# Softmax denominators in a cross attention with heads of 64: VectorE folds the sums of exps to 64 partitions, and one product takes two chunks of heads

## The chip, the cores and the metric

The kernel runs on one core of one Trainium2 chip. Its engines work side by side, each through its own queue in order: TensorE (PE in the profile; PEld is its weight load), VectorE (DVE), ScalarE (ACT), GpSimd (POOL) and SyncE (SP), which here issues DMAs. The metric is the device time of one execution in microseconds (us), the median of several runs. Everything is computed in fp32.

## The reference, cut to what matters

A decoder of two layers works on x of 8 batches, 256 tokens and 256 features. Each layer adds a self attention, a cross attention over a context of 256 rows by 512 features, and a routed feed-forward part. The change lies in the cross attention of the second layer, which has 16 heads of 64 and one more key and value, the same for every head and batch ("null"):

```python
q = _split_heads(jnp.einsum('bnd,df->bnf', x, Wq))          # x is layer-normed
kv = jnp.einsum('bmc,cf->bmf', context, Wkv)
k, v = jnp.split(kv, 2, axis=-1)
k, v = (_split_heads(k), _split_heads(v))
k = jnp.concatenate((nk, k), axis=-2)                       # nk, nv: null_kv, broadcast
v = jnp.concatenate((nv, v), axis=-2)
q = q * scale
sim = jnp.einsum('bhid,bhjd->bhij', q, k)
attn = jax.nn.softmax(sim, axis=-1)
out = jnp.einsum('bhij,bhjd->bhid', attn, v)
out = out.transpose(0, 2, 1, 3).reshape(b, -1, INNER)
out = jnp.einsum('bnf,fd->bnd', out, Wout)                  # then a layer norm with scale and bias
```

The denominator of the softmax, for each head and query, is the sum over 256 keys of exp(score), plus the exp of the null key's score.

## The kernel before

The stage is the function `null_cross_attention`, one entry per batch (the loop `for b in range(B)` at L1473). The 16 heads lie as eight chunks (`nc8`) of two heads, `g` = 0 and 1, 64 features each. Two chunks make a block, so an entry has four blocks; `c2` counts chunks in steps of two.

**Inside `weighted` (L1331).** For a chunk, `exp_scores` makes the scores transposed, keys on the partitions: PE multiplies `kT` and `qT` into `stx` (L1339; 256 keys are two tiles of 128, `kt`), ScalarE takes the exp into `pTx` (L1343), and GpSimd adds the two key tiles (L1345), so that `both` holds, on 128 partitions, sums of two keys' exps, for two heads by 256 queries. What is left is a sum over the 128 partitions. PE does it (`sums`, L1353): for each head a product with weights `hot8[:, c, :]`, a matrix of 128 by 64 that is 1 in column c and 0 elsewhere, so that the sum lands in row c of the tile `den`; rows 0 to 63 take the heads with g = 0, rows 64 to 127 those with g = 1, and the eight chunks accumulate into one PSUM tile. So an entry has 16 of these products, 128 x 64 weights and 256 columns each; the profile counts two records to a product.

The block loop (L1367) keeps PE ahead: it issues the scores of block c2 + 2, then `sums` of block c2 - 2, then the products of the exps with the values (`ox`, L1377) of block c2. `ox` is copied out of PSUM into `oT` by ScalarE for c2 = 0 and 4 and by VectorE for c2 = 2 and 6 (L1385). The last block's `sums` are left over as `rest`.

**After it.** PE transposes the next entry's normed x and the routed rows' (`tr`, L283), and makes the next entry's keys, values and queries with the seven-product scheme `seven` (L1239; k7, v7 and q7 are generators whose every `next` issues a piece of products, their sums and copies). `rest` stands behind the first piece of k7 (L1503). Then `reciprocals` (L1394): VectorE adds the null key's exp to den (`rx`) and takes the reciprocal, four DMAs on SyncE write it to DRAM and read it back spread over the partitions (`rs`), GpSimd multiplies `oT` by it (`divide`, L1428), and PE multiplies by `Wout` (`wo`).

**Buffers.** `pTx` has four, `both` has four, the PSUM tag `mm` three (ox, tr, the z tiles of `seven`, wo and nps take them in turn), `sc` two of two banks (scores and `seven`), and `den` the one bank of `op`. `oT` has one.

**Who sets the order.** The order on every engine is that of a scheduler that follows the program with its dependences; from L1493 to the end of an entry (`manual_schedule`) PE keeps the order as written. In the entries before the last two the second layer norm of an entry is made one entry ahead (`xn`), beside that of the routed rows (`xne`), which VectorE and GpSimd do at the beginning of an entry (L251 to L260).

Of the kernel before, what the change touches and what calls it, by code (L numbers as in the profile page):

```python
# [28 lines left out]
F32 = mybir.dt.float32  # L29
# [4 lines left out]
ALU = mybir.AluOpType  # L34
# [4 lines left out]
P = 128  # L39
B, S, D = 8, 256, 256  # L40
# [4 lines left out]
XH, XD = 16, 64  # L45
# [110 lines left out]
def plain(  # L156
# [4 lines left out]
    nc = tc.nc  # L161
# [402 lines left out]
    work = first.enter_context(tc.tile_pool(name="aw", bufs=2))  # L564
# [200 lines left out]
    nc8 = XH // 2  # L765
# [26 lines left out]
    def tables_x(wd, wq_x, wout_x, nkrow, nvcol):  # L792


        wn = wd.tile([P, 2, 2, XD], F32, name="wn")
        nc.gpsimd.memset(wn, 0.0)
        for k in range(2):
            byk = work.tile([P, XH, XD], F32, tag="pT", name="byk", bufs=4)
            nc.vector.tensor_tensor(
                byk,  # L800
                wq_x[:, k, :].rearrange("p (h d) -> p h d", d=XD),
                nkrow.unsqueeze(1).to_broadcast([P, XH, XD]),
                ALU.mult,
            )
            nc.vector.tensor_reduce(
                wn[:, k, :, :nc8], byk.rearrange("p (c g) d -> p g c d", g=2), AX.X, ALU.add
            )

        own = wd.tile([P, 2], F32, name="own")
        nc.vector.tensor_reduce(own, ident.rearrange("p (g w) -> p g w", g=2), AX.X, ALU.add)  # L810
        nc.vector.tensor_tensor(own, own, nvcol.to_broadcast([P, 2]), ALU.mult)
        nvs = work.tile([P, nc8, P], F32, tag="pT", name="nvs", bufs=4)
        nc.gpsimd.memset(nvs, 0.0)
        for c in range(nc8):
            nc.vector.tensor_copy(nvs[:, c, c : c + XD + 1 : XD], own)
        nvw = wd.tile([P, D], F32, name="nvw")
        ps = mm.tile([P, 2, S], F32, tag="mm", name="nvw")
        for c in range(nc8):
            nc.tensor.matmul(ps[:, 0, :], nvs[:, c, :], wout_x[:, c, :], start=c == 0, stop=c == nc8 - 1)
        nc.vector.tensor_copy(nvw, ps[:, 0, :])  # L820

        hot = wd.tile([P, nc8, XD], F32, name="hot8")
        nc.gpsimd.memset(hot, 0.0)
        nc.gpsimd.memset(hot.rearrange("p c w -> p (c w)")[:, 0 : nc8 * XD : XD + 1], 1.0)
        return wn, nvw, hot

    def beside(n):
# [15 lines left out]
    before = units[0].prepare()  # L843
# [13 lines left out]
    for n, u in enumerate(units):  # L857
        done = n
        if n == 1:
            expert_tables()  # L860
        if n == 3:
            slot_tables()
        if n == 2:
            nc.sync.dma_start(wqkv1, a["l1_wqkv"].rearrange("(c p) f -> p c f", p=P))
            nc.sync.dma_start(wo1, a["l1_wo"].rearrange("(c p) f -> p c f", p=P))
            nc.sync.dma_start(sin1, a["sin_halves"].rearrange("(t p) d -> p t d", p=P))
        if n + 2 < len(units):
            units[n + 2].load()

        if n + 1 < len(units) and units[n + 1].__class__ is SelfAttention and units[n + 1].layer == 1:  # L870
            while len(ready) <= units[n + 1].b // 2:
                next(experts_at)
        if n == len(units) - 1:
            wd, ctxs, wproj, wkv_x, wq_x, wout_x, nkrow, nvcol, lns, lnb = wx
            wn, nvw, hot8 = tables_x(wd, wq_x, wout_x, nkrow, nvcol)
        side = beside(n)
        m = (units[n - 1].pieces[1] if n else 0) + (units[n + 1].pieces[0] if n + 1 < len(units) else 0)
        made = 0
        for i, _ in enumerate(u.core()):
            while made < min(m, -(-m * (i + 1) // 7)):  # L880
                next(side)
                made += 1
            next(experts_at, None)
        for _ in side:
            pass
        opening.close()
        if len(ready) == B // 2 and wx is None:
            wx = weights_x()
# [281 lines left out]
    def null_cross_attention(phase):  # L1170
        work = phase.enter_context(tc.tile_pool(name="d2", bufs=2))
# [156 lines left out]
            nc.scalar.activation(en, nps[:, 0, :], AF.Exp, scale=scale)  # L1328
            return en

        def weighted(kT, v, qT):  # L1331


            def exp_scores(c):
                st = scp.tile([P, 2, 2, S], F32, tag="sc", name="stx")
                for kt in range(2):
                    for g in range(2):
                        rows = slice(XD * g, XD * (g + 1))
                        nc.tensor.matmul(  # L1339
                            st[:, g, kt, :], kT[rows, c, bass.ts(kt, P)], qT[rows, c, :], start=True, stop=True  # L1340
                        )
                pT = work.tile([P, 2, 2, S], F32, tag="pT", name="pTx", bufs=4)
                nc.scalar.activation(pT, st, AF.Exp, scale=scale)  # L1343
                both = work.tile([P, 2, S], F32, tag="both", name="both", bufs=4)
                nc.gpsimd.tensor_tensor(both, pT[:, :, 0, :], pT[:, :, 1, :], ALU.add)  # L1345
                return pT, both

            oT = work.tile([P, nc8, S], F32, tag="oT", name="oT", bufs=1)
            den = op.tile([P, S], F32, tag="o", name="den")

            def sums(c, both):
                for g in range(2):
                    nc.tensor.matmul(  # L1353
                        den[XD * g : XD * (g + 1), :],
                        hot8[:, c, :],
                        both[:, g, :],
                        start=c == 0,
                        stop=c == nc8 - 1,
                        skip_group_check=True,
                    )  # L1360

            def block(c2):
                return [exp_scores(c2 + i) for i in range(2)]


            ahead, before = block(0), []
            for c2 in range(0, nc8, 2):  # L1367
                now = ahead
                if c2 + 2 < nc8:
                    ahead = block(c2 + 2)  # L1370
                for i, both in enumerate(before):
                    sums(c2 - 2 + i, both)
                o = mm.tile([P, 2, S], F32, tag="mm", name="ox")
                for i, (pT, _) in enumerate(now):
                    for kt in range(2):
                        for g in range(2):
                            nc.tensor.matmul(  # L1377
                                o[XD * g : XD * (g + 1), i, :],
                                v[:, kt, 2 * (c2 + i) + g, :],
                                pT[:, g, kt, :],  # L1380
                                start=kt == 0,
                                stop=kt == 1,
                                skip_group_check=True,
                            )
                (nc.vector.tensor_copy if c2 % 4 else nc.scalar.copy)(oT[:, c2 : c2 + 2, :], o)  # L1385
                before = [both for _, both in now]

            def rest():
                for i, both in enumerate(before):
                    sums(nc8 - 2 + i, both)  # L1390

            return oT, den, rest

# [67 lines left out]
        _, xnT = layernorm_T(0, work, mm, 1)  # L1461
        ctxT, kT, v, qT = context(0), key_room(), value_room(), query_room()
# [10 lines left out]
        for b in range(B):  # L1473
            more = b + 1 < B
            if more:
                ctxT = context(b + 1)
            oT, den, rest = weighted(kT, v, qT)
            if more:
                _, xnT = layernorm_T(b + 1, work, mm, 1)
                if b:  # L1480
# [15 lines left out]
            if more:  # L1496
                of_x = sums_of_rows(xnT, 1, "swq", True)
                kT, v, qT = key_room(), value_room(), query_room()
                k7 = seven("k7", of_ctx, w_terms(kv_blocks, 0), kT, False)
                v7 = seven("v7", of_ctx, w_terms(kv_blocks, 1), v, True)  # L1500
                q7 = seven("q7", of_x, w_terms(q_blocks, 0), qT, False)
                next(k7)
                rest()  # L1503
            rs, old = reciprocals(b, den, en), en
            if b == 1:
                in_range()
# [2 lines left out]
                routing_tables(late)  # L1509
            if more:  # L1510

                for made in (k7, k7, v7, k7, k7, k7, v7, v7, q7, v7, q7, v7, v7, q7):
                    next(made)
            else:
                first = hidden_shared(0, pair, lambda n: spare()[:, 0, :n])
                for i in range(4):
                    next(first)
                    if i == 0:
                        routed_scores(b - 1)
                shared["of_w"] = sums_of_shared(*(sums.tile([P, full * P], F32, name=f"tws{i}") for i in range(4)))  # L1520
# [1242 lines left out]
```

## Time and profile before

| what | us |
|---|---|
| median of 3 runs (1362.37 to 1363.51) | 1363.12 |
| the profiled execution, its own time | 1360.92 |
| its span, first to last instruction | 1359.2 |
| first entry of the stage (650.69 to 710.01) | 59.32 |
| entries two to seven, each | 59.81 or 59.82 |
| PE busy in the third entry (769.83 to 829.64) | 59.49 of 59.81 |
| VectorE, ScalarE, GpSimd busy in it | 20.13, 17.99, 19.49 |
| L1353, all den products (256 records) | 34.3, 386 ns one record |
| L1345, all adds of GpSimd (64) | 82.0, 1308 ns one |

Times of instructions are given as they stand in the timeline: start from the beginning of the span, length, engine, line, operation, what is written from what is read, the shape, and how many were joined to one line; a bracket at the end says how long the engine was idle before, and what ended that. PE's matmuls are pipelined, so a line's length runs over into the next line's, and what a group costs is read from start to start. The TensorE clock that was granted is 0.996 of full speed over the span.

### The profile page before, as it was taken

The numbers are of one execution on the slowest core, as the hardware profiler recorded it, in microseconds if no ns is written. First come the engines' busy times: TensorE is split into PE (matmuls) and PEld (weight loads), VectorE is DVE, ScalarE is ACT, GpSimd is POOL, SyncE is SP. The second block draws the span as 40 slices with busy tenths as digits, with TensorE's granted clock in tenths as the row PEclk, the third lists the DMA queues.
The fourth block names the chain that finished last, engine by engine and source line by source line (L and its number), as shares of the span: only waits on it lengthen the run. The fifth ranks groups of instructions, "written<-read, shape, count | busy, mean of one in ns | idle before, by whom it ended". The sixth has DMA issues, their size and how long they took to land.

```text
span 1359.2 us, 30873 instructions
## 1 busy us (share of the span) xinstructions
PE 1325.6 (98%) x13180; PEld 918.7 (68%) x13180; DVE 562.6 (41%) x1622; ACT 477.5 (35%) x768; POOL 385.3 (28%) x481
## 2 busy tenths in 40 slices
PE   6999999999999999999999999999999999999998
PEld 3666766766766756665767676676767657788884
DVE  5343463463465655344333323242332547322223
ACT  2455544444444333431323323132332323022221
POOL 4232052052034244220324324141433512300004
PEclk8999999999999999999999999999999999999999
DMA  9970010000000005000111010201101111689954
GB/s 310 341 234 11 15 25 7 11 25 1 1 9 1 2 10 194 18 1 9 27 30 33 17 33 17 48 13 37 33 16 33 65 32 44 260 351 398 400 195 127
DMA packets 46930, 116.71 MB, mean 86 GB/s; under 512 B 8272, under 2 KB 30400, under 8 KB 42432
## 3 DMA queue, kind: packets, MB, share of 16 engines
q1 hardware_dynamic: 38912, 92.74, 20.2%
q0 software_dynamic: 5152, 18.89, 3.8%
q10 hardware_dynamic: 2720, 3.02, 0.6%
q8 instruction: 106, 1.74, 0.5%
q14 instruction: 40, 0.33, 0.1%
HBM read 104.00 MB, written 27.93 MB: 97 GB/s over the span
## 4 chain that ended last, share of the span: by engine, by line
PE 86%; DVE 4%; issue 2%; POOL 2%; ACT 1%; DMA 1%; SPq 0%; ACTq 0%; POOLq 0%; DVEq 0%
PE st L334 11%; PE o L366 10%; PE h L274 6%; PE v L274 6%; PE k L274 5%; PE wo L274 4%; PE ox L1377 4%; PE stx L1339 4%; PE qk L274 3%; PE out L1751 3%; PE out L1568 3%; PE h L961 3%; PE tr L283 3%; PE q L274 2%; PE den L1353 2%
## 5 line engine op out<-in xcount | busy, mean ns | idle before, releaser
L366 PE MATMUL o<-pT,padv 128*64 128x256 f32 (+1 forms) x1536 | 171.6, 365 | 1.2 <-POOL pT L346 1.2
L343 ACT ACTIVATE pT<-st 128x1024 f32<-128x1024 f32 (+1 forms) x128 | 110.5, 915 | 88.9 <-PE st L334 88.1
L366 PEld LDWEIGHTS o<-pT,padv 128*64 128x64 f32 x1536 | 103.1, 137 | 52.7 <-issue 9.6
L334 PE MATMUL st<-qm,kT 64*128 64x256 f32 (+1 forms) x1024 | 117.2, 367 | 0.9 <-DVE qm L312 0.6
L334 PEld LDWEIGHTS st<-qm,kT 64*128 64x128 f32 x1024 | 90.1, 189 | 26.2 <-issue 15.8
L1345 POOL TENSOR_TENSOR both<-pTx 128x512 f32<-128x512 f32 x64 | 82.0, 1308 | 46.0 <-ACT pTx L1343 38.9
L274 PE MATMUL h<-xrT,w 128*64 128x128 f32 (+1 forms) x1936 | 87.1, 250 | 1.4 <-issue 1.4
L274 PEld LDWEIGHTS h<-xrT,w 128*64 128x64 f32 x1936 | 84.6, 137 | 4.1 <-issue 2.0
L343 ACT ACTIVATE pT<-st,kbias 128x1024 f32<-128x1024 f32 x64 | 68.0, 1112 | 28.8 <-PE st L334 28.7
L1343 ACT ACTIVATE pTx<-stx 128x1024 f32<-128x1024 f32 x64 | 62.1, 1021 | 42.3 <-PE stx L1339 40.3
L256 POOL TENSOR_TENSOR lnrs<-lnve,mhalf 128x2 f32<-128x2 f32 x48 | 34.2, 715 | 146.0 <-DVE lnve L254 95.1
L954 DVE TENSOR_TENSOR midr<-sl,h 128x128 f32<-128x128 f32 x102 | 29.4, 288 | 101.3 <-PE h L274 67.0
L334 PE MATMUL st<-qm,memk 64*128 64x256 f32 x512 | 68.8, 393 | 0.4
L953 ACT ACTIVATE sl<-h 128x128 f32<-128x128 f32 (+1 forms) x114 | 35.3, 310 | 95.7 <-PE h L274 56.7
L1339 PE MATMUL stx<-qTx,kTx 64*128 64x256 f32 x512 | 64.3, 391 | 2.5 <-ACT pTx L1343 2.5
L274 PE MATMUL qk<-l_wqkv,xnT 128*64 128x512 f32 x256 | 62.6, 610 | 0.7 <-ACT xnT L286 0.7
L346 POOL TENSOR_SCALAR_AFFINE_SELECT pT<-pT 128x512 f32<-128x512 f32 x64 | 39.6, 638 | 80.9 <-ACT pT L343 77.6
L1377 PE MATMUL ox<-pTx,vx 128*64 128x256 f32 x512 | 61.1, 381 | 0.0
L1339 PEld LDWEIGHTS stx<-qTx,kTx 64*128 64x128 f32 x512 | 46.1, 186 | 20.3 <-ACT pTx L1343 7.2
L274 PE MATMUL wo<-wout_x,oT 128*64 128x256 f32 x512 | 58.0, 379 | 0.0
L334 PEld LDWEIGHTS st<-qm,memk 64*128 64x128 f32 x512 | 48.0, 186 | 14.8 <-issue 4.7
L1428 POOL TENSOR_TENSOR oT<-oT,rs 128x512 f32<-128x512 f32 x30 | 37.2, 1272 | 64.4 <-DMA rs<-rd 64.4
(368 smaller groups left out, 2270.1 us busy)
## 6 DMA issues: line engine op xcount, KB each, us to landing
w<-packs SPq DMA_DIRECT2D x22, 1408.0 KB
w<-packs SPq DMA_DIRECT2D x22, 768.0 KB
rs<-rd SPq DMA_DIRECT2D x16, 512.0 KB
packs<-L_ffn_w_eDF SPq DMA_DIRECT2D x8, 704.0 KB
packs<-L_ffn_w_eDF SPq DMA_DIRECT2D x8, 640.0 KB
packs<-L_ffn_w_eFD SPq DMA_DIRECT2D x8, 640.0 KB
ctxT<-ctx_T SPq DMA_DIRECT2D x8, 512.0 KB
wkv_x<-L_xattn_Wkv POOLq DMA_DIRECT2D x1, 4096.0 KB, 15.4
```

What stands on the lines that cost most here:

```text
L274: nc.tensor.matmul(out[h], lhsT[:, h], rhs, start=start, stop=stop, skip_group_check=True)
L283: nc.tensor.transpose(ps[:, c, t * P : (t + 1) * P], rows[:, t, c * P : (c + 1) * P], ident)
L334: nc.tensor.matmul(st[:, g, i, :n], kT[rows, c, bass.ts(kt, P)], qm[rows, 2 * mq + i, c, q0:], start=True, stop=True,)
L343: nc.scalar.activation(pT[:, :, :, :n], st[:, :, :, :n], AF.Exp, scale=scale, **kb)
L366: nc.tensor.matmul(o[64 * i : 64 * i + 64, mq, q0:], v_pad[:, kt, 4 * c + 2 * mq + i, 2 * g : 2 * g + 2, :], pTs[kt][:, g, i, : S - q0], s ...
L961: nc.tensor.matmul(h, shared["ws13"][:, c, lo : lo + P], shared["xnT"][:, c, bass.ts(q, 2 * S)], start=c == 0, stop=c == 1)
L1339: nc.tensor.matmul(st[:, g, kt, :], kT[rows, c, bass.ts(kt, P)], qT[rows, c, :], start=True, stop=True)
L1343: nc.scalar.activation(pT, st, AF.Exp, scale=scale)
L1345: nc.gpsimd.tensor_tensor(both, pT[:, :, 0, :], pT[:, :, 1, :], ALU.add)
L1377: nc.tensor.matmul(o[XD * g : XD * (g + 1), i, :], v[:, kt, 2 * (c2 + i) + g, :], pT[:, g, kt, :], start=kt == 0, stop=kt == 1, skip_group ...
L1568: nc.tensor.matmul(ps, mid[:, i, lo : lo + P], w2[:, i, :], start=i == 0, stop=i == NFC - 1)
L1751: nc.tensor.matmul(ps[h], mid[:, i, h], sets[k % len(sets)][1][:, i, :], start=i == 0, stop=i == NFC - 1, skip_group_check=True,)
```

## The change

Three things change in `weighted` and around it; the last entry (`folds` = `more` = False) is kept as it was but for the names of its buffers.

1. In the first seven entries VectorE adds the lower 64 partitions of `both` to the upper 64. The first chunk of a block goes to partitions 0 to 63 of a tile `folded`, the second to 64 to 127, so one `folded` holds a block of two chunks.
2. One product per head and block then takes both chunks: the weights `hot[1]` have 1 in one column for the lower 64 partitions and in the next column for the upper 64. That makes 8 products an entry instead of 16, of the same shape. The tables become a strip of 72 columns, of which each product reads a window of 64.
3. The products of a block are issued one block of scores later: behind the scores of block c2 + 2 stand now those of block c2 - 4. Two blocks are left over at the end; `rest` is called twice, behind the first and behind the second piece of k7.

`both` has two buffers instead of four, and `folded` three. In the last entry the chunks of a block take a buffer of `both` and one of `folded`, without a fold.

```diff
-        hot = wd.tile([P, nc8, XD], F32, name="hot8")
-        nc.gpsimd.memset(hot, 0.0)
-        nc.gpsimd.memset(hot.rearrange("p c w -> p (c w)")[:, 0 : nc8 * XD : XD + 1], 1.0)
+        hot = [wd.tile([P, XD + nc8], F32, name=f"hot{i}") for i in range(2)]
+        for v in hot:
+            nc.gpsimd.memset(v, 0.0)
+        nc.gpsimd.memset(hot[0][:, nc8 - 1 : nc8], 1.0)
+        for i in range(2):
+            nc.gpsimd.memset(hot[1][XD * i : XD * (i + 1), nc8 - 2 + i : nc8 - 1 + i], 1.0)
...
-        def weighted(kT, v, qT):
+        def weighted(kT, v, qT, folds):
...
-                both = work.tile([P, 2, S], F32, tag="both", name="both", bufs=4)
+                return pT
+
+            def room(odd):
+                if odd:
+                    return work.tile([P, 2, S], F32, tag="folded", name="folded", bufs=3)
+                return work.tile([P, 2, S], F32, tag="both", name="both", bufs=2)
+
+            def add(pT, both):
                 nc.gpsimd.tensor_tensor(both, pT[:, :, 0, :], pT[:, :, 1, :], ALU.add)
-                return pT, both
+                return both
+
+            def sum_block(pTs):
+                if not folds:
+                    return [add(pT, room(i)) for i, pT in enumerate(pTs)]
+                folded = room(1)
+                for i, pT in enumerate(pTs):
+                    both = add(pT, room(0))
+                    nc.vector.tensor_tensor(folded[XD * i : XD * (i + 1)], both[:XD], both[XD:], ALU.add)
+                return [folded]
...
-            def sums(c, both):
-                for g in range(2):
-                    nc.tensor.matmul(
-                        den[XD * g : XD * (g + 1), :],
-                        hot8[:, c, :],
-                        both[:, g, :],
-                        start=c == 0,
-                        stop=c == nc8 - 1,
-                        skip_group_check=True,
-                    )
+            def sums(c2, of):
+                for i, v in enumerate(of):
+                    at = nc8 - (2 if folds else 1) - c2 - i
+                    for g in range(2):
+                        nc.tensor.matmul(
+                            den[XD * g : XD * (g + 1), :],
+                            hot[folds][:, at : at + XD],
+                            v[:, g, :],
+                            start=c2 + i == 0,
+                            stop=c2 + 2 == nc8 and i + 1 == len(of),
+                            skip_group_check=True,
+                        )
...
-            ahead, before = block(0), []
+            ahead = block(0)
+            made = [(0, sum_block(ahead))]
             for c2 in range(0, nc8, 2):
                 now = ahead
                 if c2 + 2 < nc8:
                     ahead = block(c2 + 2)
-                for i, both in enumerate(before):
-                    sums(c2 - 2 + i, both)
+                if c2 >= (4 if folds else 2):
+                    sums(*made.pop(0))
+                if c2 + 2 < nc8:
+                    made.append((c2 + 2, sum_block(ahead)))
                 o = mm.tile([P, 2, S], F32, tag="mm", name="ox")
...
             def rest():
-                for i, both in enumerate(before):
-                    sums(nc8 - 2 + i, both)
+                sums(*made.pop(0))
...
-            oT, den, rest = weighted(kT, v, qT)
+            oT, den, rest = weighted(kT, v, qT, more)
...
-                next(k7)
-                rest()
+                for _ in range(2):
+                    next(k7)
+                    rest()
...
-                for made in (k7, k7, v7, k7, k7, k7, v7, v7, q7, v7, q7, v7, v7, q7):
+                for made in (k7, v7, k7, k7, k7, v7, v7, q7, v7, q7, v7, v7, q7):
                     next(made)
```

More of the change, by code (lines that the diff above doesn't have):

```diff
@@ L874, in plain @@
             wd, ctxs, wproj, wkv_x, wq_x, wout_x, nkrow, nvcol, lns, lnb = wx
-            wn, nvw, hot8 = tables_x(wd, wq_x, wout_x, nkrow, nvcol)
+            wn, nvw, hot = tables_x(wd, wq_x, wout_x, nkrow, nvcol)
         side = beside(n)
@@ L1370, in weighted @@
                     ahead = block(c2 + 2)
-                for i, both in enumerate(before):
-                    sums(c2 - 2 + i, both)
+                if c2 >= (4 if folds else 2):
+                    sums(*made.pop(0))
+                if c2 + 2 < nc8:
+                    made.append((c2 + 2, sum_block(ahead)))
                 o = mm.tile([P, 2, S], F32, tag="mm", name="ox")
-                for i, (pT, _) in enumerate(now):
+                for i, pT in enumerate(now):
                     for kt in range(2):
@@ L1385, in weighted @@
                 (nc.vector.tensor_copy if c2 % 4 else nc.scalar.copy)(oT[:, c2 : c2 + 2, :], o)
-                before = [both for _, both in now]
             def rest():
-                for i, both in enumerate(before):
-                    sums(nc8 - 2 + i, both)
+                sums(*made.pop(0))
             return oT, den, rest
```

## The prediction

> **What bounds the kernel now.** The page's head and first part come first.
>
> ```profile
> span 1359.2 us, 30873 instructions
> PE 1325.6 (98%) x13180; PEld 918.7 (68%) x13180; DVE 562.6 (41%) x1622; ACT 477.5 (35%) x768; POOL 385.3 (28%) x481
> ```
>
> PE is busy all the way, so each product that is really taken away is worth its issue time, unless PE then finds something unready. The change touches one stage, the eight entries of cross attention with heads of 64, so next I read PE's timeline in one steady entry (the third; it starts at 769.83 and the fourth at 829.64, and entries two to seven are alike within 0.01 us).
>
> ```profile
> 776.00 2.00 PE L1339 MATMUL stx<-qTx,kTx 64*128 64x256 f32 x16
> 777.93 1.08 PE L1353 MATMUL den<-both,hot 128*64 128x256 f32 x8
> 778.84 1.90 PE L1377 MATMUL ox<-pTx,vx 128*64 128x256 f32 x16
> 780.67 2.00 PE L1339 MATMUL stx<-qTx,kTx 64*128 64x256 f32 x16
> 782.60 1.08 PE L1353 MATMUL den<-both,hot 128*64 128x256 f32 x8
> 783.51 1.90 PE L1377 MATMUL ox<-pTx,vx 128*64 128x256 f32 x16
> 785.24 1.03 PE L1353 MATMUL den<-both,hot 128*64 128x256 f32 x8
> 786.10 1.90 PE L1377 MATMUL ox<-pTx,vx 128*64 128x256 f32 x16
> 787.93 0.66 PE L283 MATMUL tr<-ident,xn 128*128 128x128 f32 x4
> ```
>
> The reader is to see starts without gaps: a den group costs 0.91, 0.91 and 0.86 us from start to start (two records to a product). Next, the two engines that the change loads, VectorE and GpSimd, in the same entry:
>
> ```profile
> 774.70 1.27 POOL L1345 TENSOR_TENSOR both<-pTx 128x512 f32<-128x512 f32 x1
> 774.77 1.36 DVE L260 TENSOR_SCALAR xne<-x,lnmv,lnrs 128x256 f32<-128x256 f32 x1 [0.68 <-POOL lnrs L256]
> 776.05 0.42 DVE L260 TENSOR_SCALAR xne<-x,lnmv,lnrs 128x256 f32<-128x256 f32 x1
> 776.80 6.18 POOL L1345 TENSOR_TENSOR both<-pTx 128x512 f32<-128x512 f32 x5
> 780.79 0.69 DVE L1385 COPY oT<-ox 128x512 f32<-128x512 f32 x1 [4.32 <-PE ox L1377]
> ```
>
> The same VectorE instruction takes 1.36 us when it starts just behind a GpSimd add, ending 0.16 after it, and 0.42 without one. The adds themselves step by (6.18 - 1.27) / 4 = 1.23. The last entry already holds what the change will bring, VectorE instructions with two inputs in SBUF during those adds:
>
> ```profile
> 1079.18 1.89 DVE L973 TENSOR_TENSOR tws<-ws 128x640 f32<-128x640 f32 x1
> 1080.36 1.84 POOL L1345 TENSOR_TENSOR both<-pTx 128x512 f32<-128x512 f32 x1
> 1081.00 1.88 DVE L973 TENSOR_TENSOR tws<-ws,tws 128x640 f32<-128x640 f32 x1
> 1082.17 1.86 POOL L1345 TENSOR_TENSOR both<-pTx 128x512 f32<-128x512 f32 x1
> ```
>
> They take turns. An add ends 1.13 after the VectorE instruction ahead of it (1081.07 to 1082.20), and the VectorE instruction 0.68 after that add (1082.88). VectorE alone does four 512-wide ones like this:
>
> ```profile
> 614.12 2.48 DVE L1217 TENSOR_TENSOR tw<-wkv_x 128x512 f32<-128x512 f32 x4
> ```
>
> That is 0.68 each, a step of 0.60 where they run on.
>
> **Part one, the products removed.** In seven entries den goes from 16 products to 8. Ahead of tr the group at 777.93 goes (0.91), and those at 782.60 and 785.24 are halved (0.43 each): 1.77. The switch from stx straight to ox costs 0.05 (the ox group at 774.12 lasts 1.88 to the next start, others 1.83), so PE wants tr 1.71 earlier, at 786.22. Behind tr the old group of 0.86 becomes two halves of 0.43: nothing. Unhindered that is 7 x 1.71 = 12.0 us.
>
> **Part two, the folds added.** Eight VectorE instructions an entry, 64 partitions by 512. Half the partitions do not make one shorter: L954 takes 690 ns at 64x512 and 686 at 128x512. So 0.68 alone. Behind a running add I scale the 0.68 of 640 elements: 0.68 x 512 / 640 = 0.55 after the add's end; the bounds are 0.55 and 0.72 (0.68 and a handover of 0.04: L1235 starts at 790.07, 0.04 after the end of L1234, which it reads). I take 0.55, since L973 is the same kind of instruction against the same adds. In the changed program's order each fold also waits for the fold ahead, so a fold behind a fold costs 0.72, at the least 0.60. The tile both has two buffers instead of four: the add of chunk c waits for the fold of chunk c - 2. After a fold, the next fold is there in 0.04, GpSimd's add only in 0.14 (L1447 at 771.32, after a L1446 that ends at 770.76 + 0.42), so I let the fold go first.
>
> **What is queued behind them.** VectorE's order becomes: two xne, folds 0 to 5, the copy of ox of chunks 2 and 3, folds 6 and 7, the copy of ox of chunks 6 and 7. The tag mm has three buffers, so tr (ox two blocks on, then tr) needs the bank of that first copy, and k7z that of the second. In the old order the first copy ran at 780.79. Followed from the rows (ends):
>
> - fold 0: the second xne ends at 776.47, VectorE starts 0.08 earlier, 777.07. Add 1, issued at 776.80: +1.13, 778.20. Add 2: +1.23, 779.43. Fold 1: +0.55, 779.98. Fold 2: +0.72, 780.70.
> - Add 3 781.83, add 4 783.06, fold 3 783.61, fold 4 784.33. PE wants fold 3 (second den) at 784.0: met.
> - Add 5 785.46, add 6 786.69, fold 5 787.24, copy (0.04 + 0.69) 787.97. With 0.05 to PE, tr starts at 788.02 instead of 786.22; before it was 787.93.
>
> The copy that PE now waits for eats 1.80 of 1.71: such an entry loses 0.09. ScalarE stays covered: exp 7 needs add 3 (781.83), and its scores come at about 781.9. The second copy ends at 790.6; k7z wants its bank at 788.02 + 3.68 - 0.43 = 791.27: met.
>
> The first and the seventh entry differ in when the adds start. In the first, at 653.03, nothing of a layer norm stands ahead: adds 0 and 1 end by 655.52, folds 0 and 1 by 656.79, and with pairs of 1.13 + 1.23 + 0.55 + 0.72 = 3.63 fold 5 ends at 664.05 and the copy at 664.78, ahead of the 667.02 at which PE wants tr. It keeps 1.71. In the seventh add 1 ends at 1016.57; fold 1 1017.84, fold 5 1025.10, copy 1025.83: tr 0.40 late, and k7z, by the second copy at 1029.46, another 0.38. It keeps 1.71 - 0.78 = 0.93. Sum: 5 x 0.09 - 1.71 - 0.93 = **-2.2 us**. Against the median of 1363.12 that is 1360.9; the profiled execution itself was 1360.92 with a span of 1359.2, 2.2 below the median, and I apply the difference, not the span.
>
> A step of 0.60 between folds instead of 0.72 would bring the copy 3 x 0.12 forward: 1.8 us in five entries, and 0.3 in the seventh. That is the low edge of this case, -4.3.
>
> [...]
>
> **Part three, denominators a block later.** The last two den products move behind k7z and half of the sw products, so rx starts at about 795.4 instead of 791.83. Behind it on VectorE, SyncE's queue and GpSimd: reciprocal, four DMAs, the product with en, four products with rs; nobody else stands in those queues then. They ended at 807.47, now at 811.1, and PE wants them at 817.7: covered with 6.6 to spare. Without that cover it would cost 3.6 an entry. The last entry keeps its instructions and order on PE and VectorE, and the tables' fills on GpSimd lie far ahead of their use (first den at 658.7): nothing for both.
>
> **Rivals.**
> 1. The folds do not hold up the adds. Adds then step by 1.23, fold 5 ends at 782.98 + 0.72, the copy at 784.43, before PE wants the bank: all of 12.0 is kept, 1351.1. For it: L1385 copies during adds at 0.69, unslowed; but it has one input, in PSUM. Against it: L973. Half-way cases lie here too. 0.15.
> 2. Strict turns: after each fold the add goes first, a pace of 0.55 + 0.14 + 1.27 = 1.96 a chunk. Fold 5 ends at 779.98 + 4 x 1.96 = 787.82, tr at 788.60, +0.67 in five entries, +0.51 in the seventh, -1.71 in the first: +2.2, 1365.3. For it: L973's own turns are of this form. Against: there the add had no wait on VectorE. 0.20.
> 3. Slower: the two engines hide nothing from each other, since both buffers are two and every handover is a wait: 0.04 + 0.68 + 0.14 + 1.27 = 2.13 a chunk. Fold 1 ends at 779.43 + 0.72, fold 5 at 788.67, tr at 789.45: +1.52 in five entries and in the seventh, -1.06 in the first: +8.1, **1371**. It decides from a pace of about 2.0 a chunk on. Against it: the 0.68 and 1.13 of L973, where the starting time is hidden. 0.18.
>
> **How the numbers follow.** 0.47 for the forecast, 1360.9 (1358.8 to 1363 on its own). What the measurement can tell from no change is 0.2%, 2.7 us: the forecast lies 0.20 on the faster side of that and 0.27 inside, rival 1 is faster, rival 2 0.12 inside and 0.08 slower, rival 3 slower. Faster 0.35, same 0.39, slower 0.26. The range leaves out most of rival 1 and of rival 3: 1354 to 1367.5.
>
> **What would show it.** Right: adds beside folds at 1.8 us or so, in pairs; L283's tr behind a gap of 1.8 us in entries two to six that ends with VectorE's oT, none in the first; wo without a wait. Wrong: adds still at 1.27 and no gap (rival 1); one fold between any two adds (2); folds ending a full 0.7 after an add (3). A GpSimd wait of wo would undo part three.

## The result, and the profile after

| what | before | after |
|---|---|---|
| median, us, side by side on one chip (10 runs each) | 1363.24 (1361.6 to 1366.87) | 1368.64 (1367.14 to 1370.18) |
| ratio, with its 95% interval | | 1.0038 [1.0028, 1.0048] |
| profiled execution, us (its span) | 1360.92 (1359.2) | 1368.88 (1367.1) |
| mean granted TensorE clock of the profile | 0.996 | 0.990 |

The change made the kernel 5.4 us slower. First the page of after:

```profile
span 1367.1 us, 30772 instructions
PE 1320.0 (97%) x13068; PEld 914.8 (67%) x13068; DVE 630.7 (46%) x1678; ACT 479.1 (35%) x768; POOL 396.6 (29%) x484
```

PE is busy for 5.6 us less, in a span that is 7.9 us longer, so it stands still for longer, and part of what it still does runs slower. The third entry shows both. In the kernel after, L1356 is GpSimd's add, L1367 the fold, L1377 the den products, L1405 ox and L1413 its copy. PE's timeline there (start, length, engine, line, operation; it starts at 768.98):

```profile
783.10 0.60 PE L1377 MATMUL den<-folded,hot 128*64 128x256 f32 x4
783.53 1.90 PE L1405 MATMUL ox<-pTx,vx 128*64 128x256 f32 x16
787.43 0.66 PE L283 MATMUL tr<-ident,xn 128*128 128x128 f32 x4 [2.01 <-DVE oT L1413]
787.93 0.87 PE L283 MATMUL tr<-ident,xne 128*128 128x128 f32 x4
788.73 3.32 PE L274 MATMUL k<-ctxT,wkv_x 128*64 128x128 f32 x32
```

PE stands still for 2.01 us ahead of tr, until VectorE's copy of ox is done; tr starts 18.45 into the entry, 0.35 later than before (18.10). And the 32 records of k behind it, which take 1.97 in an entry that runs at full clock, take 3.32. The table by stretches says why. Its columns are the stretch, its length, the busy time with the instructions in brackets of PE, PEld, DVE, ACT and POOL, then the granted clock, the DMA share and GB/s:

```profile
784.70:788.12 3.42, 1.41 (x14) 0.89 (x11) 3.14 (x3) 0.00 (x0) 2.67 (x3) 1.00 0.00 0
788.12:791.53 3.41, 3.41 (x30) 3.08 (x30) 3.24 (x9) 1.17 (x2) 0.00 (x0) 0.50 0.00 0
...
907.58:911.00 3.42, 1.46 (x14) 0.71 (x10) 2.43 (x2) 0.00 (x0) 2.73 (x3) 1.00 0.01 2
911.00:914.41 3.41, 3.37 (x47) 3.06 (x49) 3.25 (x6) 1.35 (x3) 0.68 (x1) 1.00 0.00 0
```

Behind the gap of the third entry the clock is 0.50 for one stretch of 3.41 us. Behind an equal gap in the fifth (909.03 to 911.04) it is not. The clock's own records have such rows at 788.12, 849.56 and 972.44 in the stage, and before had none there (its granted clock is 1.00 in each of the seven entries). They lie a multiple of 3.413 us apart (61.44 is 18 x 3.413, 122.88 is 36 x 3.413), so the stretches stand on a fixed grid. Each row makes an entry 1.6 us longer, as the lengths show (from an entry's first stx to the next one's):

```
entry         first  second  third  fourth  fifth  sixth  seventh    sum
before        59.32   59.82  59.81   59.82  59.82  59.82    59.82  418.2
after         57.59   60.21  61.79   61.82  60.17  61.85    59.23  422.7
```

The first entry keeps 1.73. The second and fifth lose 0.37, which is the wait; third, fourth and sixth lose 2.0, of which 1.6 is the clock; the seventh gains 0.59. The sum is +4.44, and without the three rows it would be about -0.5 (5 x 0.37 - 1.73 - 0.59); the rows make up 4.9. The ten timed runs of after carry the same sign: their mean clock is 0.990 to 0.993, that of before's thirteen runs beside the first experiments 0.993 to 0.996, and one row of 0.5 is 3.41 x 0.5 / 1367 = 0.00125 of it. The other 3.4 us between the two spans lie outside the entries: 0.5 ahead of them (a row of 0.5 at 610.62 may have a part in it; the stage starts anywhere from 648.93 to 652.17 in the profiles of all versions), 0.3 later, and 2.7 behind PE's last matmul. The profiled execution of before was 2.3 below the median of its runs, so its end is not compared here. By the medians the loss is 5.4: the stage accounts for 4.44 of it, and about 1.0 is not traced.

VectorE and GpSimd in the third entry of after, in two views:

```profile
777.51 2.54 DVE L1367 TENSOR_TENSOR folded<-both 64x512 f32<-64x512 f32 x2 [1.16 <-POOL both L1356]
781.22 2.54 DVE L1367 TENSOR_TENSOR folded<-both 64x512 f32<-64x512 f32 x2 [1.17 <-POOL both L1356]
784.92 1.74 DVE L1367 TENSOR_TENSOR folded<-both 64x512 f32<-64x512 f32 x1 [1.17 <-POOL both L1356]
786.69 0.69 DVE L1413 COPY oT<-ox 128x512 f32<-128x512 f32 x1
```

```profile
775.96 2.75 POOL L1356 TENSOR_TENSOR both<-pTx 128x512 f32<-128x512 f32 x2
779.40 3.02 POOL L1356 TENSOR_TENSOR both<-pTx 128x512 f32<-128x512 f32 x2 [0.69 <-DVE folded L1367]
783.11 3.00 POOL L1356 TENSOR_TENSOR both<-pTx 128x512 f32<-128x512 f32 x2 [0.69 <-DVE folded L1367]
```

Two adds, two folds, two adds: each pair waits for the other engine's, 3.70 us for two chunks (777.51 to 781.22, 781.22 to 784.92). A record of 1.74 is not a slow fold: it starts with the add still running and ends 0.55 after it. The copy of ox stands behind all of this, although its data were there long before (it ran at 10.96 into an entry before, at 17.7 now).

### The profile page after: what moved, and what is told of

Read it like the earlier page. It is cut to its first block, busy times and chain, and to the rows that moved or that the text cites. A ratio compares the mean times of both kernels' runs of the same rounds, so it can differ in the third digit from the quotient of the medians.

```text
span 1367.1 us, 30772 instructions
## 1 busy us (share of the span) xinstructions
PE 1320.0 (97%) x13068; PEld 914.8 (67%) x13068; DVE 630.7 (46%) x1678; ACT 479.1 (35%) x768; POOL 396.6 (29%) x484
## 3 DMA queue, kind: packets, MB, share of 16 engines
q8 instruction: 105, 1.72, 0.5%
## 5 line engine op out<-in xcount | busy, mean ns | idle before, releaser
L1356 POOL TENSOR_TENSOR both<-pTx 128x512 f32<-128x512 f32 x60 | 86.0, 1449 | 53.5 <-ACT pTx L1347 38.9
L1367 DVE TENSOR_TENSOR folded<-both 64x512 f32<-64x512 f32 x56 | 65.3, 1167 | 28.5 <-POOL both L1356 25.7
L1405 PE MATMUL ox<-pTx,vx 128*64 128x256 f32 x512 | 61.5, 382 | 0.0
```

Source lines behind the costliest of these rows:

```text
L1367: nc.vector.tensor_tensor(folded[XD * i : XD * (i + 1)], both[:XD], both[XD:], ALU.add)
L1405: nc.tensor.matmul(o[XD * g : XD * (g + 1), i, :], v[:, kt, 2 * (c2 + i) + g, :], pT[:, g, kt, :], start=kt == 0, stop=kt == 1, skip_group ...
```

## The experiments

Ratios are to the kernel before, measured beside each version on the same chip. Absolute times of different experiments are not compared, since the kernel before took 1359.4 to 1362.9 beside them; where an expectation gives microseconds, the ratio times 1363.24 (before's time beside the changed kernel) is set against it. Four questions: is it the copy's place in VectorE's queue, is it the turns that VectorE and GpSimd take, is it the clock, and is it the later place of the den products.

**Take the copies from VectorE.**

```diff
-(nc.vector.tensor_copy if c2 % 4 else nc.scalar.copy)(oT[:, c2 : c2 + 2, :], o)
+nc.scalar.copy(oT[:, c2 : c2 + 2, :], o)
```

> All four copies of ox in an entry go to ScalarE; folds, adds and products stay as in the changed kernel. Theory Q (queue): the loss is the copy of ox that stands on VectorE behind six folds, each taking its turn with an add on GpSimd (1.86 us a chunk); PE idles 2.0 us ahead of tr in entries 2 to 6 and in some of them the granted clock is 0.5 for the 3.41 us after. Then tr goes when PE is free, about 1.7 us earlier than before in all seven entries, no clock row of 0.5 is left inside the span, and the time is 1351.5 us (1350 to 1354). Theory S (sums): the adds themselves, 1.86 us apart in place of 1.34, hold up the scores or the k products by their buffers, whoever copies: 1362 to 1369. Theory D (denominators): the products of den taken later, or the moved rest, cost the time: 1366 to 1369.

Measured 1351.75, ratio 0.9917 [0.9898, 0.9936]. The entries are 57.59 and six times 58.09, 12.1 less than before in sum, and the clock has no row of 0.5 in the stage. PE's timeline in the third entry:

```profile
779.18 0.60 PE L1377 MATMUL den<-folded,hot 128*64 128x256 f32 x4
779.61 1.90 PE L1405 MATMUL ox<-pTx,vx 128*64 128x256 f32 x16
781.44 0.66 PE L283 MATMUL tr<-ident,xn 128*128 128x128 f32 x4
781.93 0.60 PE L283 MATMUL tr<-ident,xne 128*128 128x128 f32 x4
782.46 1.97 PE L274 MATMUL k<-ctxT,wkv_x 128*64 128x128 f32 x32
```

No bracket anywhere: tr goes 16.38 into the entry. The folds and adds are as slow as in the changed kernel (fold 7 still starts 19.70 into the entry), so their pace by itself costs nothing here, and theories S and D fall. Once more, for a tighter interval:

> The kernel with all copies of ox on ScalarE once more, for a tighter ratio and another profile. Theory Q: 0.9915 of before (0.990 to 0.993), seven entries 1.73 us shorter each, no row of 0.5 inside the stage. Rival (the first such run stood on a good chip): above 0.995.

Ratio 0.9925 [0.9911, 0.9938], again 57.59 and six times 58.09. This version beats both kernels.

**Change the order in the program.**

```diff
-                if c2 + 2 < nc8:
-                    made.append((c2 + 2, sum_block(ahead)))
                 o = mm.tile([P, 2, S], F32, tag="mm", name="ox")
...
                 (nc.vector.tensor_copy if c2 % 4 else nc.scalar.copy)(oT[:, c2 : c2 + 2, :], o)
+                if c2 + 2 < nc8:
+                    made.append((c2 + 2, sum_block(ahead)))
```

> Order alone: the folds and adds of the next block are issued behind the copy of ox of this block, so VectorE's first copy stands behind four folds, not six; nothing else differs from the changed kernel. Theory Q: fold 3 ends about 14.0 us from the entry's first stx and the copy 14.7, and tr is wanted at 16.4: no wait there; the second copy still stands behind folds 6 and 7 (about 21.2), which k7z wants at about 21.4: at most a few tenths in an entry. 1353 us (1351 to 1357), no 0.5 clock row. Theories S and D: as the changed kernel, 1366 to 1369.

Ratio 1.0058 [1.0042, 1.0075]. The expected 1353 was missed, and the run doesn't test theory Q: the scheduler gave VectorE the order that it had, six folds, the copy, two folds, the copy, with the copy again at 17.72 into the entry. It serves as a second sample of the changed kernel, and there too three of five gaps of 2.0 us are followed by a row of 0.5.

**Leave the folds out.**

```diff
-                folded = room(1)
-                for i, pT in enumerate(pTs):
-                    both = add(pT, room(0))
-                    nc.vector.tensor_tensor(folded[XD * i : XD * (i + 1)], both[:XD], both[XD:], ALU.add)
-                return [folded]
+                add(pTs[0], room(0))
+                return [add(pTs[1], room(1))]
```

> Leaves out the eight folds of an entry: the eight products of den take the odd chunk's sums as they are (the even chunk's sums are made and not read), so the denominators are not the reference's. What is left is half the products, taken a block later. Theories Q and S: 7 x 1.71 = 12.0 us less than before, 1351 us (1349.5 to 1353), tr without a gap. Theory D: 1362 to 1369, with waits at the den products or at k7z.

The whole time, 1468.65, says nothing: other denominators send other tokens to the experts, and PE has 13410 matmuls against 13068. The stage can be read: 57.60 and six times 58.09, to 0.01 the entries of the run with ScalarE's copies. So the halved products are worth 1.73 an entry, and with the copies on ScalarE the folds cost nothing of it.

**More buffers for the adds.**

```diff
-                    both = add(pT, room(0))
+                    both = add(pT, room(0) if i else folded)
```

> The first sum of a pair is made in the folded tile (3 buffers) and folded in place, the second in both (2 buffers): five buffers for the adds in place of two, in the same space. [...] Theory B (buffers): the turns are forced by an add's wait for the fold two before it; with more buffers the adds go on 1.3 us apart, the folds fall behind by themselves and the copy of ox goes elsewhere: a different pace in the trace and 1357 to 1365 us.

Ratio 0.9979 [0.9968, 0.9989], 57.59, five entries of 59.5 and 58.93. The time is in theory B's range (1360.4 by the ratio), but the adds don't go on 1.3 apart, and the 1.85 of the changed kernel is not there either. VectorE's and GpSimd's views, third entry:

```profile
776.99 1.57 DVE L1367 TENSOR_TENSOR folded<-folded 64x512 f32<-64x512 f32 x1
778.67 1.58 DVE L1367 TENSOR_TENSOR folded<-both 64x512 f32<-64x512 f32 x1
```

```profile
776.29 1.72 POOL L1356 TENSOR_TENSOR both<-pTx 128x512 f32<-128x512 f32 x1
777.98 1.73 POOL L1356 TENSOR_TENSOR folded<-pTx 128x512 f32<-128x512 f32 x1
```

Now they change turns after every instruction, at 1.68 us a chunk: the add at 777.98 ends 1.15 behind the fold ahead of it (778.56, 779.71), the next fold 0.54 behind that add (780.25). The turns are there with five buffers too, but having only two costs 0.17 a chunk more (3.70 / 2 against 1.68). tr's gap is 1.35 us, no row of 0.5 appears in the stage, and the change wins a little.

**Fill the gap with work, and leave the wait.** The last four matmuls of ox are made twice.

```diff
-                for i, pT in enumerate(now):
+                last = [(1, now[1])] if folds and c2 + 2 == nc8 else []
+                for i, pT in list(enumerate(now)) + last:
```

> As the changed kernel, and in the seven entries the last four matmuls of ox (one chunk) are made twice, with the same values, ahead of tr: the wait stays, but 0.43 us of it is filled with work. Theory C (clock): a stretch of 3.41 us on a fixed grid in which TensorE stands idle for 2.0 us or more is followed by one at half clock, which costs 1.6 us; with 1.57 us of idle time left there is none. tr starts where it did (18.45 us from the first stx in entries 2 to 6), no clock row of 0.5 inside the stage, 1368.6 - 3 x 1.6 + 0.5 = 1364.3 us (1362.5 to 1366). Theory W (the wait alone): the rows of 0.5 are chance or have another cause, and more work can't make it faster: 1368.5 to 1370.5, rows of 0.5 as before.

Ratio 1.0001 [0.999, 1.0012]. PE, third entry (it starts at 769.68):

```profile
784.23 2.76 PE L1406 MATMUL ox<-pTx,vx 128*64 128x256 f32 x24
788.14 0.65 PE L283 MATMUL tr<-ident,xn 128*128 128x128 f32 x4 [1.15 <-DVE oT L1414]
788.63 0.60 PE L283 MATMUL tr<-ident,xne 128*128 128x128 f32 x4
789.16 1.97 PE L274 MATMUL k<-ctxT,wkv_x 128*64 128x128 f32 x32
```

The filling was 0.86 us rather than 0.43. tr starts 18.46 into the entry, as in the changed kernel, with the same wait for the same copy; only the idle time is 1.15, not 2.01. No gap is followed by a row of 0.5, k takes 1.97, and the entries are 58.46, five of 60.2, 59.22: 0.4 over before in sum. It is not a lucky profile alone: the ten timed runs have a mean clock of 0.995 to 0.998, against 0.990 to 0.993 in the changed kernel. More work on the busiest engine made the kernel faster (1.0001 against 1.0038), and 1363.4 by the ratio is in theory C's range. Theory W falls.

**A shorter and a longer gap.** ScalarE copies one chunk of the bank, then VectorE copies the bank twice.

```diff
+                if folds and c2 == 2:
+                    nc.scalar.copy(oT[:, c2 + 1, :], o[:, 1, :])
+                    nc.vector.tensor_copy(oT[:, c2, :], o[:, 0, :])
+                else:
...
```

> As the changed kernel, but ScalarE copies one of the two chunks in VectorE's first copy of ox, so that VectorE's part is 256 columns, not 512: about 0.3 us less, and a gap of 1.7 us ahead of tr. Theory C: no clock row of 0.5, 1368.6 - 4.8 - 5 x 0.3 = 1362.3 us (1360.5 to 1364). Theory W: 1368.6 - 1.5 = 1367.1 us (1366 to 1368.5).

Ratio 1.0007 [0.9996, 1.0018], which is 1364.2 on the forecast's scale, between the theories (the 1361.41 itself was measured beside a before of 1359.4): gaps of 1.75 to 1.77, and behind the last two of the five a row of 0.5. Theory C's bound of 2.0 us of idle time is wrong, and theory W's 1367.1 is missed too. The stretches with the first and the fourth gap:

```profile
722.17:725.58 3.41, 1.64 (x16) 0.90 (x13) 2.44 (x3) 0.00 (x0) 2.72 (x3) 1.00 0.00 0
903.08:906.49 3.41, 1.66 (x20) 1.26 (x18) 3.35 (x3) 0.73 (x2) 2.19 (x2) 1.00 0.00 0
```

The same busy time, and only the second is followed by half clock (906.49). What differs is the work: 1.39 of ox and 0.26 of tr in the first, 0.24 of ox, 1.09 of tr and 0.33 of k in the second.

```diff
+                if folds and c2 == 2:
+                    nc.vector.tensor_copy(oT[:, c2 : c2 + 2, :], o)
```

> As the changed kernel, but VectorE makes its first copy of ox twice, which lengthens the gap ahead of tr to 2.7 us in entries 2 to 6 and makes one of 1.3 us in the seventh. Theory C: every stretch of the grid with 2.0 us or more of idle time in it is followed by a row of 0.5, and no other; three to five of the five: 1368.6 + 6 x 0.67 + 0 to 2 x 1.6 = 1372.6 to 1375.8 us. Theory W: 1372.6 us, and rows of 0.5 that don't follow the idle time.

Ratio 1.006 [1.0037, 1.0082], 1371.4 on the forecast's scale and less than either theory had. Gaps of 2.82 to 2.85, two rows of 0.5, behind 2.85 and 2.50 us of idle time in one stretch; none behind 2.01 (twice), with 1.41 and 1.40 of ox beside it. Again the idle time alone doesn't decide.

**Take the den products as early as before**, on the version with ScalarE's copies.

```diff
-                if c2 >= (4 if folds else 2):
+                if c2 >= 2:
...
-                for _ in range(2):
-                    next(k7)
-                    rest()
+                next(k7)
+                rest()
+                next(k7)
```

> All copies of ox on ScalarE as in the run that took the copies from VectorE (1351.75 us), and the products of den issued as early as before the change: a block sooner, the last one behind the first k product. Theory P (place): they then wait for folds 3 and 5, which end 14.0 and 17.7 us into an entry and are wanted at about 12 and 14; ox of the last block and tr stand behind them, tr comes at about 20 in place of 16.4, and in several entries a gap of 2 us or more brings rows of 0.5: 1375 to 1390 us. Rival: the place of the products doesn't matter, 1351.5 us (1350 to 1353.5).

Ratio 1.0064 [1.004, 1.0087]: about 20 us more than with the products a block later (0.992), so without the later place even ScalarE's copies don't make the folds pay. The size was less than theory P expected, and the wait stands at the first group already, for fold 1. PE, second entry (from 709.14):

```profile
715.32 2.00 PE L1343 MATMUL stx<-qTx,kTx 64*128 64x256 f32 x16
719.48 0.65 PE L1377 MATMUL den<-folded,hot 128*64 128x256 f32 x4 [2.16 <-DVE folded L1367]
719.96 3.31 PE L1405 MATMUL ox<-pTx,vx 128*64 128x256 f32 x16
```

The 3.31 of ox is a row of 0.5 (720.28); two more stand at 781.72 and 966.04. Here a row makes an entry only 0.64 longer (61.97 against 61.33): in the fourth and fifth entry, which have none, PE waits another 0.81 us for a later fold, and with a row that wait is gone. So a row cost 1.6 in the changed kernel, where nothing else was waiting, and 0.64 here.

**Change which copies VectorE makes.**

```diff
-(nc.vector.tensor_copy if c2 % 4 else nc.scalar.copy)(oT[:, c2 : c2 + 2, :], o)
+(nc.scalar.copy if c2 % 4 else nc.vector.tensor_copy)(oT[:, c2 : c2 + 2, :], o)
```

> As the changed kernel, but the copies of ox change engines: VectorE takes the first and third (queued behind four and behind eight folds), ScalarE the second and fourth. Theory Q (queue): the wait goes to whoever needs the bank of the copy behind the folds: tr goes at once (16.4 to 16.6), and k7z, which takes the third copy's bank, waits for it until about 21.1 in place of 19.6 in entries 2 to 6, a gap of about 1.4 us and no clock row of 0.5; first entry -1.7, seventh -0.9, the others -0.2 each: 0.9974 of before (0.996 to 0.999). Rival (ScalarE's order, not the folds, let the run without VectorE's copies win): 1.003 to 1.005, as the changed kernel, with the gap ahead of tr.

Ratio 1.0213 [1.0197, 1.0229]: right that the wait goes to whoever needs that bank, wrong about who, and far from both figures (0.9974, and 1.003 to 1.005 for the rival). PE, second entry (from 706.53), then the stretches in the third:

```profile
723.28 0.66 PE L283 MATMUL tr<-ident,xn 128*128 128x128 f32 x4
727.75 1.11 PE L283 MATMUL tr<-ident,xne 128*128 128x128 f32 x4 [3.81 <-DVE oT L1413]
```

```profile
787.42:790.84 3.42, 1.39 (x12) 0.72 (x8) 2.20 (x2) 1.17 (x2) 2.99 (x2) 1.00 0.00 0
790.84:794.25 3.41, 1.61 (x10) 1.28 (x12) 3.15 (x9) 0.46 (x1) 0.00 (x0) 0.50 0.00 0
794.25:797.67 3.42, 3.42 (x34) 3.23 (x32) 0.00 (x0) 0.33 (x2) 0.00 (x0) 0.50 0.00 0
```

The two tr tiles are two banks: the second, not k7z, takes that of the third copy, which stands behind all eight folds. The gap of 3.8 leaves 1.39 and 1.61 us of PE work in two stretches, the stretch behind each runs at 0.50, and an entry grows from 58.09 (all copies on ScalarE) to 64.87: 3.8 of gap, about 2.6 of clock, 0.36 of ox waiting for the first copy's bank.

## Why the prediction was wrong, step by step

Forecast 1360.9 (-2.2), measured 1368.64 (+5.4): above the range too.

- **Part one**, PE wants tr 1.71 earlier: right. 1.73 in each of the seven entries where nothing holds it (folds left out, copies on ScalarE). Its own terms, 1.77 - 0.05, make 1.72.
- **Part two**, the turns: right in kind. Pairs of adds and folds, ending 1.13 and 0.55 behind each other, a gap ahead of tr in entries two to six that VectorE's oT ends, none in the first, a short one (0.58) in the seventh. A pair of pairs takes 3.70 and not 3.63, since a fold starts 0.10 behind the fold ahead and not 0.04, and the first fold ended 0.13 later: it started 0.03 behind the end of xne (775.63, 775.66) and not 0.08 before it. So the copy ended at 18.40 into the entry and not at 18.14. "Such an entry loses 0.09" should have been 0.37, and the seventh keeps 0.59, not 0.93. That term is 1.7 us too small (5 x 0.28 + 0.34), so the stage would have been at -0.5. The measured size lies on the way to rival 2 (+2.2), but its picture of one fold between any two adds is not what ran with two buffers.
- **The step that failed** is "The copy that PE now waits for eats 1.80 of 1.71: such an entry loses 0.09". The gap of 1.80 us was priced at its length alone. In three of the five entries the gap of 2.0 us also cost clock, 1.6 us each, 4.9 in all, and the mis-sized wait only 1.7; the remaining 1.0 of the 7.6 us between forecast and measurement is not found in the profile's seven entries and is not traced. The run with useless work in the gap shows it: tr goes as late as in the changed kernel, the rows of 0.5 are gone, and the ratio is 1.0001. The profile of before held no such row behind a gap, and none of its gaps in these entries reached 0.4 us (the longest, 0.38, at 708.12); no rival had it.
- **Part three**: right. rx starts at 796.45, GpSimd's products with rs end at 807.24 + 4.96 = 812.20, in an entry with a row of 0.5, and wo starts at 818.82 without a wait. The 6.6 to spare came out as 818.82 - 812.20 = 6.6. But the later place does more than it was given there: taken as early as before, with ScalarE's copies, the same products cost about 20 us, since they then wait for the folds.
- **The fold by itself.** A fold, whose inputs lie on partitions 0 to 63 and 64 to 127, took 0.69 us with no add beside it (788.72 to 789.41 in the third entry), as long as the copy (0.69), against the 0.68 forecast. Its start is late, though: a fold starts 0.10 behind the end of the fold ahead (782.97, 783.07), where xn starts 0.08 before the end of the copy ahead (790.13, 790.05). So it ends 0.79 behind the fold ahead (782.97 to 783.76); the 0.72 of the sum was an estimate from other instructions. The step of 0.60 behind the low edge did not come; what makes the 0.10 no run separates.
- **Rival 1** (1351.1) named the prize, and one line away from the change it is there (1351.75 and 1351.30), though not by its mechanism. The folds do hold up the adds (1.85 us a chunk against 1.23); but nothing that PE waits for has to stand behind them.

## What to carry over

When work is added to an engine that is mostly idle, look at what else stands in its queue and who waits for that: here 5.5 us of VectorE's own work an entry (8 x 0.69) were free, and one copy behind them was not. Move the short instruction that frees a bank to an engine whose queue is clear before counting how fast the added work can be. A gap on TensorE can cost more than its length, as three of five gaps of 2.0 us did here by 1.6 us each: look at the granted clock of the stretch behind it, and ask whether several short gaps, or filler, are cheaper than one long one.

## What the runs showed of the hardware

- The clock's grid. Over these profiles, a stretch of 3.413 us of the grid that held only products of stx, den or ox was followed by one at 0.5 when they took 1.30 us or less (0.92, 1.25, 1.27, 1.30), and not when they took 1.40 or more (1.40, 1.41, 1.43, 1.45, 1.52, 1.56; the 1.45 is the 1.46 of the table, whose stretch is a little wider). The bound is read off these profiles; no run was made to test it. With transposes in it, stretches of 1.44 and even 1.66 us of busy time were followed by one at 0.5; so busy time alone doesn't decide (1.41 of ox alone was not followed by such a row, 0.73 of ox with 0.68 of tr was). What part transposes and k have in it stays open; no run varied them alone. The entries of after are 57.59 to 61.85 long, none of them a multiple of 3.413, so their gaps fall at different places on the grid, and which gaps are hit changes from run to run: those of entries three, four and six in after, of three, four and five in the version with the same order on VectorE.
- The size of the gap. 2.0 us of idle time was followed by a row of 0.5 in three of five entries (after), 1.75 to 1.77 us in two of five (ScalarE copying one chunk of the bank); where the gaps were 1.35 us (five buffers) and 1.15 us (useless work in the gap) no row of 0.5 followed.
- An add and a fold on the two engines end in turns, together 1.68 us a chunk (the version with five buffers; alone an add took 1.27 and a fold 0.69), while a copy from PSUM on VectorE (0.69) and an add (1.26) run beside each other unslowed (786.69 and 786.80 in after; the copy with no add beside it, at 789.44, took 0.69 too).
